# The seam between two layers of an attention and convolution kernel: the last head kept by quarters of partitions, one root table, a program order on three engines

## The chip, the cores and the metric

The kernel runs on one core of a Trainium2 chip, in float32. The metric is the device time of one execution in microseconds. A measurement is the median of several runs.

## The reference, cut to what matters

The input x has two images of 256 channels and 64 x 64 pixels. Two layers are applied, each to the group-normalised input (32 groups of 8 channels), and each is added to its input:

```python
x = x + layer0(_gn(x))
x = x + layer1(_gn(x))

def layer0(x):                      # attention over 4096 pixels, 8 heads of 32 channels
    q, k, v = qkv_w @ x + qkv_b
    return softmax(q.T @ k / sqrt(32)) @ v      # per head

def layer1(x):
    q, k, v = conv1 @ x + b1, conv2 @ x + b2, conv3 @ x + b3
    fq, fk = q / 8 + pos, k + pos
    # "lr": attention inside each of 64 blocks of 64 pixels taken 8 apart, then a 1x1 conv (lr_W), scale, shift, relu
    feats = relu(lr_W @ attention(blockify(fq), blockify(fk), blockify(v)) * scale + shift)
    # "sr": attention inside each 8x8 patch, behind two 1x1 convs with relu for q and k, sr_fv for v, sr_W after
    out_att = relu(sr_W @ attention(qx(feats), kx(feats), sr_fv @ feats) * scale + shift)
    # a 3x3 convolution of q, k and v, mixed by fc_w and dep_w
    out_conv = conv3x3(fc_w, dep_w, (q, k, v))
    return rate1 * out_att + rate2 * out_conv
```

The second group norm needs the mean and variance of the finished output of layer 0, all heads of a group of 8 channels and all pixels.

## The kernel before

The two images are worked one after the other (b = 0, 1). The 256 channels lie as two chunks (k = 0, 1) of 128 partitions, and the 4096 pixels as 8 tiles of 512; `xts[t]` holds tile t of x as 128 x 2 x 512.

*Attention of layer 0 (`attention0`).* A head and a half of the queries make a group g, 16 groups per image. Within a group a loop runs over 32 key blocks j, each with four units of 512 queries. For each unit PE computes scores (L438), ACT takes the exponential (L444), and PE multiplies by the values (L454). The four units of a group lie on four quarters of the partitions, 32 channels each. The sums of the exponentials over the keys are kept partly by adds on DVE (L491, tiles `e`), partly by adds in memory through DMAs that POOL issues (L501, `acc`). For the last group two more units (`SUMMED_LAST`) are left to PE, which adds up all of them over the partitions in the matmuls named `rows`. Earlier groups send their sums through DRAM (`dsum`, `dense`, `drec`) to be inverted and spread again, and send their result to `ctx0` in DRAM, from where `add_output` fetches it and adds it to x with the bias. PE, ACT and DVE run here in the order of the program (`tc.manual_schedule`). Elsewhere a scheduler orders engines by its own due times, apart from PE, whose order is by hand through the layer 1 code as well. `at_block(g, j, ...)` hangs a piece of work onto a block of this loop; `wanted` is a list of pieces that need a spare score bank in PSUM.

*The seam.* `finish_last` handles the last group without DRAM: reciprocal of `rows` (L557), then for each quarter a multiply (L563) and an add to x (L565) on 32 partitions. `Stats` makes the group norm: `bn_stats` by tile (L268), aggregation (L272), one matmul with a group matrix for the mean (`pm_l`, L273), four small DVE steps, one matmul for the variance (`pv_l`, L281), a square root on ACT (L282) and a reciprocal. For chunk 0 this happens at blocks 6 and 9 of the last group, for chunk 1 behind the last head. The square root and the exponential lie in different tables of ACT.

*The first part of layer 1 (`layer1_first`).* `to_groups` writes the normalised x in block order into `xg` (L980 on ACT, L295 on DVE). Chunk 0 is projected by PE first (L1011), then chunk 1, then position terms (L1015), for tile 0; then eight tiles of the block attention follow (scores `sp_lr` L910, values `pvs_lr` L893, `pc_lr` L948). For b = 0 `fold_products` multiplies two pairs of weight matrices first (transposes L208, copies L209, products L213, copies L216), and `conv_weights` prepares the weights of the convolution on DVE (L724 to L764, tile `prep`), stored by SP to `wf_kept` in DRAM (L766).

*The second part (`layer1_second`).* Tile by tile: the 8 x 8 attention (L1104, L1112, L948) and the convolution, whose weights are fetched from `wf_kept` (L781, `wf`) and for b = 0 turned by PE once (`pw`, L790). The convolution's matmuls are `mm` (L831).

*Buffers.* `w4` is a pool of 11 tiles of one size that all stages share. `es` (part of a ring of exponentials, and `acc[0]`), `xg` and `xp` share a single place, one after the other. `prep` and `wf` share another. [...]

Of the kernel before, what the change touches and what calls it, by code (L numbers as in the profile page):

```python
# [40 lines left out]
def direct_layers(ctx: ExitStack, tc: tile.TileContext, a: dict, out: bass.AP, bad: bass.AP):  # L41
# [17 lines left out]
    def w4(shape, name, dtype=F32):  # L59
        return work.tile(shape, dtype, tag="w4", name=name)  # L60
# [56 lines left out]
    nc.gpsimd.dma_start(out=bv0, in_=a["bv0"].rearrange("(k p) -> p k", p=P))  # L117

    wts = {}

# [56 lines left out]
    def stack_positions(t):  # L177
# [14 lines left out]
        return halves_of  # L192

    def fold_products():


        outer = {}
        wts["fv"] = w4([P, KC, C], "wt_fv")
        nc.gpsimd.dma_start(out=wts["fv"], in_=a["fv"].rearrange("(k p) m -> p k m", p=P))
        for name in ("lr", "srw"):  # L200
            outer[name] = w4([P, KC, C], "wt_" + name)
            nc.gpsimd.dma_start(out=outer[name], in_=a[name].rearrange("(k p) m -> p k m", p=P))
        for name, behind in (("w3", "lr"), ("fv", "srw")):
            turned = w4([P, KC, C], "turned_" + name)
            for j in range(KC):
                pt = bank([P, C], f"pt_{name}_{j}")
                for k in range(KC):
                    nc.tensor.transpose(pt[:, k * P : (k + 1) * P], wts[name][:, k, j * P : (j + 1) * P], ident)  # L208
                nc.vector.tensor_copy(turned[:, j, :], pt)  # L209
            for k in range(KC):  # L210
                pt = bank([P, C], f"pm_{name}_{k}")
                for j in range(KC):
                    nc.tensor.matmul(  # L213
                        pt, turned[:, j, k * P : (k + 1) * P], outer[behind][:, j, :], start=j == 0, stop=j == KC - 1
                    )
                nc.scalar.copy(wts[name][:, k, :], pt)  # L216
            nc.sync.dma_start(out=kept_w[name], in_=wts[name])
        pt = bank([P, KC], "pb_lr")
        for m in range(KC):
            for j in range(KC):  # L220
                nc.tensor.matmul(
                    pt[:, m : m + 1], outer["lr"][:, j, m * P : (m + 1) * P], wts["b3"][:, j : j + 1],
                    start=j == 0, stop=j == KC - 1,
                )
        moved = small.tile([P, KC], F32, tag="gn_d", name="moved")
        nc.vector.tensor_mul(moved, pt, vecs[:, V_LR : V_LR + 2])
        nc.vector.tensor_add(vecs[:, V_LR + 2 : V_LR + 4], vecs[:, V_LR + 2 : V_LR + 4], moved)


# [24 lines left out]
    class Stats:  # L254
# [11 lines left out]

        def tile(self, k, t):
            nc.vector.bn_stats(self.stats[:, k, t, :], self.xts[t][:, k, :])  # L268

        def means(self, ks, pm):  # L270
            for k in range(ks.start, ks.stop):
                nc.vector.bn_aggr(self.mv[:, k, :], self.stats[:, k].rearrange("p t s -> p (t s)"))  # L272
            nc.tensor.matmul(pm, group8, self.mv[:, ks, 0], start=True, stop=True)  # L273
            d = self.d[:, ks]
            nc.vector.tensor_copy(self.mean[:, ks], pm)
            nc.vector.tensor_sub(d, self.mv[:, ks, 0], self.mean[:, ks])
            nc.vector.tensor_mul(d, d, d)
            nc.vector.tensor_add(d, d, self.mv[:, ks, 1])

        def deviations(self, ks, pv):  # L280
            nc.tensor.matmul(pv, group8, self.d[:, ks], start=True, stop=True)  # L281
            nc.scalar.activation(self.rstd[:, ks], pv, AF.Sqrt, bias=eps)  # L282
            nc.vector.reciprocal(self.rstd[:, ks], self.rstd[:, ks])

    def group_stats(xts, tagn):
        st = Stats(xts, tagn)
        for t in range(NT):
            for k in range(KC):
                st.tile(k, t)
        st.means(slice(0, KC), bank([P, KC], f"pm_{tagn}"))  # L290
        st.deviations(slice(0, KC), bank([P, KC], f"pv_{tagn}"))
        return st.mean, st.rstd

    def normalise(dst, src, k, mean, rstd):
        nc.vector.tensor_scalar(dst, src, mean[:, k : k + 1], rstd[:, k : k + 1], ALU.subtract, ALU.mult)  # L295

# [97 lines left out]

    SUMMED_LAST = (NJ - 2, NJ - 1)

    def attention0(b, xts, held):
# [116 lines left out]
        def sum_rows(g, rows):  # L514
            if g == last:
                quarters(rows, ones, lambda u: acc[u], True, False)
                for j in SUMMED_LAST:
                    quarters(rows, ones, lambda u: unit(g, j, u), False, False)
            quarters(rows, ones, lambda u: added[g][u // 2][:, u % 2, :], g < last, True)
# [30 lines left out]
        def finish_last(g):  # L550

            h, p = divmod(g, 2)
            rows = psum["sc"].tile([P, 3, T], F32, tag="sa", name=f"rows_{b}")[:, 0, :]
            sum_rows(g, rows)
            avs = copied[g]
            kept = w4([P, T], f"kept_{b}")
            nc.vector.reciprocal(avs[:, 1, :], rows)  # L557
            nc.scalar.copy(kept, rows)
            row, c = slice(HD0 * (h % 4), HD0 * (h % 4) + HD0), h // 4
            o = [w4([P, 2, T], f"o_{b}_{g}_{w}") for w in range(2)]  # L560
            for u in range(4):
                q = slice(HD0 * u, HD0 * u + HD0)
                nc.vector.tensor_mul(o[u // 2][row, u % 2, :], avs[q, 0, :], avs[q, 1, :])  # L563
                xs = xts[4 * p + u][row, c, :]
                nc.vector.scalar_tensor_tensor(xs, o[u // 2][row, u % 2, :], bv0[row, c : c + 1], xs, ALU.add, ALU.add)  # L565

# [4 lines left out]

            return check

# [17 lines left out]
        def at_block(g, j, what):  # L591
            also.setdefault((g, j), []).append(what)
# [16 lines left out]
        wanted = []  # L609
        at_block(last, 6, lambda: wanted.append(lambda bank: st.means(first_chunk, bank[:, 0:1])))  # L610
        at_block(last, 9, lambda: wanted.append(lambda bank: st.deviations(first_chunk, bank[:, 0:1])))
        rests = {}
# [42 lines left out]
        with tc.manual_schedule(engines={E.PE, E.Activation, E.DVE}):  # L655
# [33 lines left out]
            assert next(work, None) is None  # L689
            return finish_last(last), st  # L690

# [271 lines left out]

    def layer1_first(b, xts, check, st):


        mean, rstd = st.mean, st.rstd

        xg = apool.tile([P, KC, 64, 8, 8], F32, tag="A", name=f"xg_{b}")
        shift = small.tile([P, KC], F32, tag="gn_shift", name=f"shift_{b}")  # L970

        def to_groups(k):
            nc.vector.scalar_tensor_tensor(
                shift[:, k : k + 1], mean[:, k : k + 1], -1.0, rstd[:, k : k + 1], ALU.mult, ALU.mult
            )
            for t in range(NT):
                dst = xg[:, k, :, t, :].rearrange("p (d e) o -> p d e o", d=8)
                src = xts[t][:, k, :].rearrange("p (d o e) -> p d e o", d=8, o=8)
                if k == 0 or t % 2:
                    nc.scalar.activation(  # L980
                        dst, src, AF.Identity, bias=shift[:, k : k + 1], scale=rstd[:, k : k + 1]
                    )
                else:
                    normalise(dst, src, k, mean, rstd)

# [36 lines left out]

        to_groups(0)
        if b == 0:
            fold_products()
        with tc.manual_schedule(engines={mybir.EngineType.PE}):
            open_tile(0)
            for m in range(KC):
                project(0, m, slice(0, 1))
            for t in range(NT):  # L1030
                st.tile(1, t)
            st.means(slice(1, KC), bank([P, 1], f"pm_l1_{b}"))
            st.deviations(slice(1, KC), bank([P, 1], f"pv_l1_{b}"))
            to_groups(1)
            check()
            for m in range(KC):
                project(0, m, slice(1, KC))
            for t in range(NT):
                def to_feats(m, pc, t=t):
# [17 lines left out]
        load_set(b, ("fq1", "fk1", "fv"))  # L1057
        if b == B - 1:
            report()
        if b == 0:  # L1060
            kept["bias"] = conv_weights()
        return feats, mean, rstd, shift

    def layer1_second(b, xts, feats, mean, rstd, shift, pacc):
# [28 lines left out]
        for t in range(NT):  # L1093
# [25 lines left out]
            with tc.manual_schedule(engines={mybir.EngineType.PE}):  # L1119
# [26 lines left out]
                if t < 2:  # L1146
                    conv()
            conv_edges(xts, t)
            results[t] = res
            for n in sorted(n for n in results if done >= 4 * (n // 2 + 1)):  # L1150
# [10 lines left out]
    for b in range(B):  # L1161
# [13 lines left out]
        with tc.tile_pool(name=f"sc_{b}", bufs=1, space=PSUM) as psum["sc"]:  # L1175
            check, st = attention0(b, xts, held)
        with tc.tile_pool(name=f"ps1_{b}", bufs=8, space=PSUM) as psum["ps"]:
            between = layer1_first(b, xts, check, st)
        with (
# [562 lines left out]
```

## Time and profile before

| | |
|---|---|
| time, median of 3 runs | 3227.35 us (3225.48 to 3230.16) |
| profiled execution, its own time | 3228.88 us |
| profiled execution, span of the instructions | 3227.1 us |
| granted clock of PE, mean | 0.984 |
| busy: PE, DVE, ACT, POOL | 3106.4, 2484.7, 2323.5, 822.5 us |

The profile gives busy time by engine, then the span in 40 slices of about 81 us each, then the groups of instructions by line. The timeline lists single instructions, with the idle time of the engine just before one in brackets and what ended it. The windows give busy time of all engines, granted clock, and DMA for a stretch.

### The profile page before, as it was taken

Reading aid. Unit: us, or ns where it says so; the run is one execution under the profiler, and the core shown is the slowest. Engines: PE = TensorE matmul, PEld = TensorE weight load, DVE = VectorE, ACT = ScalarE, POOL = GpSimd, SP = SyncE. Lnnn points to the kernel's source line nnn. Section 1 sums busy time; section 2 is a strip of 40 time slices with the busy share of each in tenths; the row PEclk is TensorE's granted clock in tenths of the full one; section 3 lists DMA queues with packets and bytes.
Section 4 is the critical chain, followed back from the end, with each engine's and each line's share of the span. In section 5 each row is a group of like instructions: output and inputs, shape, how many; then the busy total and the mean of one; then the engine's idle time right before and its main releaser. Section 6 shows DMA issues by size and latency. Waiting matters only on the chain. (4 is left out here: it accounts for less than half of the span.)

```text
span 3227.1 us, 62236 instructions
## 1 busy us (share of the span) xinstructions
PE 3106.4 (96%) x24873; PEld 1843.5 (57%) x24873; DVE 2484.7 (77%) x3230; ACT 2323.5 (72%) x2368; POOL 822.5 (25%) x913
## 2 busy tenths in 40 slices
PE   7999999999999969999998999999999999799998
PEld 4455555555555535667654555555555555356765
DVE  4699998999999888564436998989989998624543
ACT  2699999999999953522326999999999999524222
POOL 2122222222222210344201222222222222004430
PEclk9999999999999979999999999999999999799999
DMA  7968879689786641300159678796897866400000
GB/s 255 259 127 172 160 157 184 140 160 179 153 179 129 134 97 50 138 27 27 53 190 256 126 168 162 154 184 139 165 178 150 177 130 134 110 3 10 20 14 21
DMA packets 241868, 425.21 MB, mean 132 GB/s; under 512 B 98752, under 2 KB 109336, under 8 KB 239136
## 3 DMA queue, kind: packets, MB, share of 16 engines
q0 software_dynamic: 96288, 241.20, 38.7%
q1 hardware_dynamic: 145280, 179.93, 20.7%
q8 instruction: 197, 3.23, 0.4%
q14 instruction: 103, 0.84, 0.1%
HBM read 118.26 MB, written 67.86 MB: 58 GB/s over the span
## 5 line engine op out<-in xcount | busy, mean ns | idle before, releaser
L491 DVE TENSOR_TENSOR e<-e,es 128x1024 f32<-128x1024 f32 (+1 forms) x956 | 1040.6, 1146 | 92.6 <-ACT es L444 91.3
L454 PE MATMUL av<-es,v 128*32 128x256 f32 (+1 forms) x9644 | 747.4, 391 | 0.0
L491 DVE TENSOR_TENSOR e<-e,v 128x1024 f32<-128x1024 f32 (+1 forms) x640 | 676.5, 1111 | 53.2 <-ACT v L444 52.0
L444 ACT ACTIVATE es<-sa 128x1536 f32<-128x1536 f32 (+1 forms) x444 | 635.6, 1432 | 94.6 <-PE sa L438 52.2
L438 PE MATMUL sa<-q,k 128*128 128x512 f32 x1736 | 561.9, 431 | 16.2 <-ACT es L444 5.5
L454 PE MATMUL av<-v 128*32 128x256 f32 (+1 forms) x6228 | 507.0, 389 | 0.0
L454 PEld LDWEIGHTS av<-es,v 128*32 128x32 f32 x9644 | 316.9, 109 | 300.4 <-issue 162.0
L438 PEld LDWEIGHTS sa<-q,k 128*128 128x128 f32 x1736 | 280.5, 188 | 299.6 <-issue 142.4
L438 PE MATMUL sc<-q,k 128*128 128x512 f32 x1180 | 373.0, 397 | 9.6 <-ACT es L444 8.3
L438 PE MATMUL sb<-q,k 128*128 128x512 f32 x1180 | 371.5, 396 | 1.7 <-ACT es L444 1.5
L454 PEld LDWEIGHTS av<-v 128*32 128x32 f32 x6228 | 216.4, 109 | 178.6 <-issue 81.6
L444 ACT ACTIVATE es<-sc 128x1024 f32<-128x1024 f32 x296 | 306.9, 1037 | 7.1 <-DMA v<-es 7.1
L444 ACT ACTIVATE es<-sb 128x1024 f32<-128x1024 f32 x296 | 302.1, 1020 | 5.0 <-DMA acc<-es 5.0
L444 ACT ACTIVATE v<-sc 128x1024 f32<-128x1024 f32 x294 | 304.9, 1037 | 0.2 <-DMA acc<-v 0.2
L444 ACT ACTIVATE v<-sb 128x1024 f32<-128x1024 f32 x294 | 300.0, 1020 | 0.4 <-DMA acc<-v 0.4
L438 PEld LDWEIGHTS sc<-q,k 128*128 128x128 f32 x1180 | 211.1, 188 | 81.6 <-ACT es L444 19.7
L438 PEld LDWEIGHTS sb<-q,k 128*128 128x128 f32 x1180 | 221.1, 188 | 57.4 <-ACT es L444 5.0
L444 ACT ACTIVATE v<-sa 128x1536 f32<-128x1536 f32 (+1 forms) x146 | 209.2, 1433 | 33.4 <-PE sa L438 13.7
L831 PE MATMUL mm<-v,wf 128*128 128x256 f32 x1024 | 229.4, 383 | 2.5 <-DVE z L840 2.5
L501 POOL DMA_DIRECT2D es<-es x118 | 101.2, 857 | 484.4 <-ACT es L444 439.8
L821 POOL TENSOR_TENSOR v<-col 128x512 f32<-128x512 f32 x128 | 162.4, 1300 | 212.0 <-PE sp_sr L910 81.7
L831 PEld LDWEIGHTS mm<-v,wf 128*128 128x128 f32 x1024 | 194.7, 191 | 36.9 <-issue 7.7
(238 smaller groups left out, 3256.6 us busy)
## 6 DMA issues: line engine op xcount, KB each, us to landing
acc<-es POOLq DMA_DIRECT2D x130, 512.0 KB, 6.4
acc<-v POOLq DMA_DIRECT2D x84, 512.0 KB, 6.3
es<-es POOLq DMA_DIRECT2D x138, 256.0 KB, 4.3
v<-es POOLq DMA_DIRECT2D x134, 256.0 KB, 5.0
k<-wk_halves SPq DMA_DIRECT2D x64, 512.0 KB
q<-wq_halves SPq DMA_DIRECT2D x256, 128.0 KB
v<-v POOLq DMA_DIRECT2D x90, 256.0 KB, 4.9
es<-v POOLq DMA_DIRECT2D x86, 256.0 KB, 4.0
```

The costliest lines, as they stand in the source:

```text
L438: nc.tensor.matmul(sc[:, i, :], held["k", g // 2][:, j * P : (j + 1) * P], held["q", g, u // 2][:, u % 2, :], start=True, stop=True,)
L444: nc.scalar.activation(dst, sc[:, i : i + m, :], AF.Exp, scale=SC0)
L454: nc.tensor.matmul(dst[HD0 * u : HD0 * u + HD0, n], lhs, rhs(u)[:, n], start=start, stop=stop)
L491: nc.vector.tensor_add(dst[:, s, :], dst[:, s, :], src)
L501: nc.gpsimd.dma_start(out=dst, in_=src, accum_op=ALU.add)
L821: (nc.gpsimd.tensor_add if plus else nc.gpsimd.tensor_sub)(dst, rows(one), rows(two))
L831: nc.tensor.matmul(mm[:, m, r, :], wf[:, k, 4 * r + q, m * P : (m + 1) * P], v[r // 2][:, r % 2, k, :], start=k == 0, stop=k == KC - 1,)
```

## The change

The last group's output stays on the four quarters of the partitions: one multiply, one add and one `bn_stats` on 128 partitions take the place of four each. For this, the x and the bias of that head are fetched once more in that arrangement (`x_last`, `bv_last`); four small copies put the statistics into place, and four copies put the sum back into x, two on POOL and two on ACT. The other tiles of chunk 1 get their `bn_stats` inside the last group. The square root of chunk 0 moves from block 9 to behind the loop. Three units, not two, are left to PE's `rows`, and their order changes. PE, ACT and DVE are ordered by hand up to the projection of tile 0. For b = 0 the weights to be multiplied are fetched by SP at block 12 of the last group, and the copies of the turned ones go from DVE to ACT. The instructions of `conv_weights` on DVE are put behind the last normalisation. `report` moves to a later stage. The diff, cut:

```diff
+    bv_last = const.tile([P, 1], F32, name="bv_last")
+    for u in range(4):
+        nc.gpsimd.dma_start(
+            out=bv_last[HD0 * u : HD0 * u + HD0, :], in_=a["bv0"][C - HD0 : C].rearrange("(p o) -> p o", o=1)
+        )
...
-    def fold_products():
+    def fetch_to_fold():
         wts["fv"] = w4([P, KC, C], "wt_fv")
-        nc.gpsimd.dma_start(out=wts["fv"], in_=a["fv"].rearrange("(k p) m -> p k m", p=P))
+        nc.sync.dma_start(out=wts["fv"], in_=a["fv"].rearrange("(k p) m -> p k m", p=P))
         for name in ("lr", "srw"):
             outer[name] = w4([P, KC, C], "wt_" + name)
-            nc.gpsimd.dma_start(out=outer[name], in_=a[name].rearrange("(k p) m -> p k m", p=P))
+            nc.sync.dma_start(out=outer[name], in_=a[name].rearrange("(k p) m -> p k m", p=P))
+
+    def fold_products():
...
-                nc.vector.tensor_copy(turned[:, j, :], pt)
+                nc.scalar.copy(turned[:, j, :], pt)
+            yield
...
-    SUMMED_LAST = (NJ - 2, NJ - 1)
+    SUMMED_LAST = (NJ - 3, NJ - 2, NJ - 1)
...
             if g == last:
-                quarters(rows, ones, lambda u: acc[u], True, False)
                 for j in SUMMED_LAST:
-                    quarters(rows, ones, lambda u: unit(g, j, u), False, False)
+                    quarters(rows, ones, lambda u: unit(g, j, u), j == SUMMED_LAST[0], False)
+                quarters(rows, ones, lambda u: acc[u], False, False)
...
         def finish_last(g):
+            nc.scalar.activation(st.rstd[:, first_chunk], st.d[:, first_chunk], AF.Sqrt, bias=eps)
...
-            for u in range(4):
-                q = slice(HD0 * u, HD0 * u + HD0)
-                nc.vector.tensor_mul(o[u // 2][row, u % 2, :], avs[q, 0, :], avs[q, 1, :])
-                xs = xts[4 * p + u][row, c, :]
-                nc.vector.scalar_tensor_tensor(xs, o[u // 2][row, u % 2, :], bv0[row, c : c + 1], xs, ALU.add, ALU.add)
+            y = avs[:, 0, :]
+            nc.vector.tensor_mul(y, y, avs[:, 1, :])
+            nc.vector.scalar_tensor_tensor(y, y, bv_last, held["x_last"], ALU.add, ALU.add)
+            some = small.tile([P, 6], F32, tag="gn_some", name=f"some_{b}")
+            nc.vector.bn_stats(some, y)
+            for u in range(4):
+                nc.vector.tensor_copy(
+                    st.stats[P - HD0 : P, 1, 4 * p + u, :], some[HD0 * u : HD0 * u + HD0, :]
+                )
+
+            def put(copy, us):
+                for u in us:
+                    copy(xts[4 * p + u][P - HD0 : P, 1, :], y[HD0 * u : HD0 * u + HD0, :])
...
-        at_block(last, 6, lambda: wanted.append(lambda bank: st.means(first_chunk, bank[:, 0:1])))
-        at_block(last, 9, lambda: wanted.append(lambda bank: st.deviations(first_chunk, bank[:, 0:1])))
+        def variance_of_first(bank):
+            st.variances(first_chunk, bank[:, 0:1])
+            nc.scalar.copy(st.d[:, first_chunk], bank[:, 0:1])
+
+        at_block(last, 5, lambda: st.aggregate(first_chunk))
+        at_block(last, 6, lambda: wanted.append(lambda bank: st.means(first_chunk, bank[:, 0:1], nc.scalar.copy)))
+        at_block(last, 11, lambda: st.spread(first_chunk))
+        at_block(last, 12, lambda: wanted.append(variance_of_first))
+
+        for t in range(NT):
+            if t < NT // 2:
+                at_block(last, 27 + t, lambda t=t: st.tile(1, t))
+            else:
+                at_block(last, 16 + t, lambda t=t: st.tile(1, t, P - HD0))
+        if b == 0:
+            at_block(last, 12, fetch_to_fold)
...
+        at_block(last, 21, fetch_x_last)
...
-        to_groups(0)
-        if b == 0:
-            fold_products()
-        with tc.manual_schedule(engines={mybir.EngineType.PE}):
+        with tc.manual_schedule(engines={E.PE, E.Activation, E.DVE}):
+            st.aggregate(second)
+            fold = fold_products() if b == 0 else iter(())
+            put(nc.gpsimd.tensor_copy, (0, 1))
+            ahead = (1, 1, 1, 1, 0) if b == 0 else (0,) * 7
+            for t, n in enumerate(ahead):
+                to_groups(0, t, True)
+                for _ in range(n):
+                    next(fold)
+                if t == (3 if b == 0 else 4):
+                    put(nc.scalar.copy, (2, 3))
+            pm, pv = bank([P, 1], f"pm_l1_{b}"), bank([P, 1], f"pv_l1_{b}")
+            st.means(second, pm, nc.vector.tensor_copy)
+            st.spread(second)
+            st.variances(second, pv)
+            st.deviations(second, pv)
+            shift_of(st, 1)
+            for t in range(len(ahead), NT):
+                to_groups(0, t, True)
+            n_act = 1 if b == 0 else 2
+            for t in range(NT):
+                done = to_groups(1, t, t < n_act)
+            for _ in fold:
+                pass
+            check()
             open_tile(0)
             for m in range(KC):
                 project(0, m, slice(0, 1))
-            for t in range(NT):
-                st.tile(1, t)
-            st.means(slice(1, KC), bank([P, 1], f"pm_l1_{b}"))
-            st.deviations(slice(1, KC), bank([P, 1], f"pv_l1_{b}"))
-            to_groups(1)
-            check()
             for m in range(KC):
                 project(0, m, slice(1, KC))
+        with tc.manual_schedule(engines={E.PE}):
...
         if b == 0:
-            kept["bias"] = conv_weights()
+            with tc.issue_after(done.ins):
+                kept["bias"] = conv_weights()
```

## The prediction

> **What bounds the kernel now.** I read the busy table first, then the slices, then the chain of waits, then the timeline of the stretches where the chain leaves PE.
>
> ```profile
> PE 3106.4 (96%) x24873; PEld 1843.5 (57%) x24873; DVE 2484.7 (77%) x3230; ACT 2323.5 (72%) x2368; POOL 822.5 (25%) x913
> PE   7999999999999969999998999999999999799998
> PEclk9999999999999979999999999999999999799999
> ```
>
> PE is the bound nearly everywhere, so only three kinds of time are for sale: PE's idle, PE running at half clock, and work put on PE. Both rows dip in slices 15 and 35, the two seams. At batch 1's seam the chain has the whole story; the timeline of the same stretch gives the lengths:
>
> ```profile
> 2771.86 9.70 ACT L980 ACTIVATE xg<-x,shift,rstd_l 128x512 f32<-128x512 f32 x8 [1.18 <-PE rows L454]
> 2773.52 3.36 DVE L557 RECIPROCAL avs<-rows 128x512 f32<-128x512 f32 x1 [1.23 <-PE rows L454]
> 2782.07 2.08 PE L1011 MATMUL pq_lr<-xg,wt_w 128*128 128x512 f32 x2 [8.62 <-ACT kept L558]
> 2784.27 0.69 DVE L268 BATCH_NORM_STATS2 stats_l<-x 128x6 f32<-128x512 f32 x1
> 2791.90 0.59 PE L273 MATMUL pm_l<-mv_l,group 128*128 128x1 f32 x2 [3.24 <-DVE mv_l L272]
> 2793.99 1.28 ACT L282 ACT_TABLE_LOAD   x1 [11.97 <-PE pv_l L281]
> 2800.91 2.08 PE L1011 MATMUL pq_lr<-xg,wt_w 128*128 128x512 f32 x2 [7.01 <-ACT xg L980]
> 2811.82 0.48 PE L910 MATMUL sp_lr<-k_lr,q_lr 128*64 128x64 f32 x4
> ```
>
> PE waits 8.62 us for eight ACT xg and kept, runs the first chunk, waits 3.24 us for the slow statistics of the last head (per quarter 0.68 + 0.75 + 0.69, one behind another), then 7.01 us for table load, sqrt and the second chunk's xg. What PE does run there is cold:
>
> ```profile
> 2784.60:2787.90 3.30, 3.30 (x5) 1.35 (x4) 3.17 (x6) 0.00 (x0) 0.00 (x0) 0.50 0.03 11
> 2801.00:2811.80 10.80, 10.80 (x12) 3.05 (x12) 0.69 (x1) 2.48 (x3) 0.00 (x0) 0.50 0.00 0
> 1344.15:1347.57 3.42, 2.93 (x27) 2.69 (x26) 2.17 (x4) 2.88 (x6) 3.34 (x4) 1.00 0.02 5
> ```
>
> The third column from the end is the granted clock. A 128x512 pass costs 0.86 us at 0.50, 0.43 at 1.00. Stepping windows, the clock drops at 2777.7, rises at 2787.9 after a 3.4 us window wholly full of projections, drops at 2791.3, and rises only at 2818.6. Batch 0 has the same shape (1163.2 down, 1180.2 up, 1190.5 down, 1214.4 up), with the weight products in between. So a seam costs its gaps twice: once as idle, once as half speed of what follows.
>
> **The change part by part** (times of the profiled execution; span 3227.1, its own time 3228.88; the median of the runs is 1.5 below that, and I subtract gains from the median).
>
> *1. Root tables.* In the last group now:
>
> ```profile
> 2730.22 1.28 ACT L282 ACT_TABLE_LOAD   x1
> 2731.82 0.96 PE L438 MATMUL sa<-q,k 128*128 128x512 f32 x3 [1.28 <-ACT rstd_l L282]
> 2735.66 0.96 PE L438 MATMUL sa<-q,k 128*128 128x512 f32 x3 [0.52 <-ACT es L444]
> ```
>
> Add a third gap of 0.18 at 2737.49: PE loses 1.98 us per batch to the pair of loads. [...] What replaces it is two tiny copies on ACT from a spare bank; the next scores wait for each, some 0.3 us (the 0.26 of the sqrt row plus a hand-over): -1.98 + 0.6 = **-1.4 us per batch**. Bounds: 0 to -2.
>
> *2. Statistics in the last group.* Eight bn_stats of 0.69 = 5.5 us more on DVE, two adds of 1.15 less, against a DVE that idled 5.15 + 1.15 us at these same matmuls. The x and fold fetches pass SP, idle between 1121 and 1131, ahead of the results of group 14. Cost 0; without that cover, the difference of 3 us.
>
> *3. Rows.* One more unit is summed by PE: 5 groups of 0.86 us, not 4: +0.86. The acc slot, which the first xg waits for, is now read in the fourth of five groups instead of the first: xg may start at 2773.6, 1.7 later than 2771.9. This speaks against the change; it is in the sum below.
>
> *4. Batch 1's seam.* DVE after rows at 2774.4: reciprocal 3.4, mul 0.7, add 0.75, bn_stats 0.7, four small copies 0.7, aggregate 0.4: 2780.8 (now 2791.8). pm, four small DVE steps, pv, as now 1.9: variance at 2782.6. ACT: one root table at 2770.7, under the rows; from 2773.6 seven xg of 1.21, kept 0.6, two copies back 1.2 (the other two on POOL; nearest row, kept's 0.56, and up to 1.3 on POOL, waited for only by the last xg), sqrt 0.3, eighth xg: first projections at about **2785.0**, 2.9 later than 2782.07. Then the gain: the second chunk's xg (six on DVE at 0.67, two on ACT) end near 2788, while PE is still in the first chunk; the waits of 3.24 and 7.01 and the 1.28 table load go. PE runs two chunks without a pause: 8 cold passes of 0.86 are 6.9; the clock should rise after the first full window (3.4 to 6.8 us from the start), and the second chunk with its position passes takes 5 to 6 us warm. sp_lr at 2795.6 to 2797.3, against 2811.82: -14.5 to -16.2. From there to the next tile is now 8.24 us, of which about 2.5 is the cold clock (sp and pvs_lr take 5.7 in a warm tile). **-17.5 us.**
>
> [...] 6.9 us hold one full window of a 3.4 us grid, barely: I take the rise, at 0.75. Without it the gain is 2.5 + 5 + 1 less: about -9.
>
> *5. Batch 0's seam and what eats it.* The weight products are woven into the same order, turned copies on ACT (0.37 each), weights fetched at block 12 and not after the rows. The first projections come at 1176 to 1180 (now 1184.5), the second chunk follows at once (now 1197.4), sp_lr at 1188 to 1193 against 1208.3. So tile 1 starts 17 to 22 us earlier. But the conv weights are made on DVE beside this stage, and the change lets them begin only after the last normalise:
>
> ```profile
> 1164.59 0.63 DVE L724 TENSOR_TENSOR prep<-prep 128x108 f32<-128x108 f32 x3 [0.61 <-DMA prep<-in_bx_dram]
> 1216.07:1324.50 108.43, 108.43 (x585) 63.44 (x585) 95.39 (x249) 41.88 (x61) 2.28 (x3) 1.00 0.18 49
> 1330.13 0.35 SPq L781 DMA_DIRECT2D wf<-wf_kept  x1
> 1342.58 2.40 PE L790 MATMUL pw<-ident,wf 128*128 128x128 f32 x20 [0.82 <-DMA wf<-wf_kept]
> ```
>
> DVE is busy 95.4 us from 1216.1 to 1324.5; softmax and bd rows are 16.9 of it, so conv weights 78.5, a rate of 0.72. Before 1216 their rows add to 28.2; they overlap (14 of 478 ns within 5.62), so 23.7. Total 102 us of DVE. After: start 1179, alone till sp at 1188 (9 us), then at 0.72 until the stage's end at 1188 + 121 = 1309 (87 us), the last 6 alone: done at 1315, now 1324.4. With sp at 1193 it is 1319. From there stores, fetch and pw take 18.2 us as now: pw at 1333 to 1337 instead of 1342.6: 5.5 to 9.5 gained of some 20. PE ends prq near 1319 to 1324 and waits 13 us for wf. In that gap it goes cold, and pw's 64 transposes (7.3 us busy, 0.11 each) run at half speed. [...] By the trace they lift it: 1.7 to 3.4 us lost. [...] I take -7.5 + 2.5: **-5 us**, ends -9 and +3. Nothing else waits: POOL's loads for prep are issued as before, the loc_lr loads stand behind the stores as now.
>
> *6. Check and report moved.* Small DVE steps (0.7, 0.2) off the path: 0; bounds 0 and 1.
>
> Sum: -1.4 x 2 - 17.5 - 5 = **-25.3**; 3227.35 - 25.3 = **3202**.
>
> **The rivals.**
> A (0.62): as above, batch 1's seam gains in full, batch 0's is mostly handed to the wait for wf: 3195 to 3209.
> B (0.20): the clock does not rise in batch 1's first chunk, or the woven products run cold and late (ACT now does turned copies, xg and pm copies in order): -2.8 - 9 - 1 = -13: about 3214. For it: the long cold stretches above. Against: two full windows in each seam did lift it.
> C (0.10): conv weights are no bound, since DVE, no longer stalled in the seam, is faster than 0.72: both seams pay, -2.8 - 17.5 - 18: about 3189. For it: DVE idles 11 us before nm, den and bd rows in that window.
> D (0.05), slower: the fold fetches. They stand in SP's queue ahead of group 14's denominators, waiting for slots that PE frees. DVE's order is fixed: if dense comes late, the reciprocals and x adds at block 26 stall the row sums behind them, and the score ring fills. Slots freed at the rows of group 14 cost nothing. Scores of seven units come every 3.5 to 3.7 us and a block has four, so a block is 2.1 us, and that is the price of each block of lateness. It decides from 12 blocks (25 us) on: held from block 12 to the group's end, 20 blocks, it costs 42, net +17: 3244. Against: SP's queue shows no wait of that kind and PE frees slots every group.
> E (0.03): the seam does not move, since xg starts later by the shared slot (part 3) and the hand order leaves ACT waiting for quarters; only part 1 stays, some -3 + 2: 3226.
>
> **How the numbers follow.** Predicted time 3202. Leaving out C's lower half, D and E and the tail of B gives 3190 to 3215. Within 0.2% is 6.5 us, about what a measurement here can tell from no change. Faster A + B + C = 0.92, same E 0.03, slower D 0.05.
>
> **What would show it.** Right: no table load around 2730 and PE's gaps there down to 0.3; bn_stats of the last head once, not four times; sp_lr of batch 1 within 27 us of the rows' end (now 38.4); no PE gap between the two chunks; the granted clock at 1.00 from before sp_lr on; in batch 0 a PE gap of 10 to 15 us ahead of pw, ended by the DMA of wf. Wrong: a gap before pm_l or before the second chunk; clock 0.50 up to pvs_lr (B); no gap ahead of pw (C); waits in group 15 (D).

## The result, and the profile after

The changed kernel takes 3211.94 us (median of 4, 3209.81 to 3213.45) against 3228.76 before in the same runs: ratio 0.9949, 95% interval 0.9931 to 0.9966, so 16.8 us faster. 3202 was forecast, with 3190 to 3215 as the range. The profiled execution has a span of 3211.4 us and a granted clock of 0.989.

The page of the changed kernel, busy table and slices:

```profile
PE 3093.3 (96%) x24889; PEld 1838.3 (57%) x24889; DVE 2487.2 (77%) x3223; ACT 2316.5 (72%) x2371; POOL 826.7 (26%) x918
PE   7899999999999989699998999999999999899998
PEclk9999999999999999899999999999999999999999
```

The dip of image 1's seam (35th slice) is an 8 instead of a 7, that of image 0's (15th) an 8 instead of a 6, and the clock's dips there are gone (9 in both slices). But the 17th slice, a 9 before, is now a 6, and the clock dips in it: an idle time has moved there. The timeline of image 1's seam, first two lines of before, then the same stretch after:

```profile
2769.84 0.59 PE L454 MATMUL rows<-es,ones 128*32 128x512 f32 x1
2820.06 1.88 PE L1011 MATMUL pq_lr<-xg,wt_w 128*128 128x512 f32 x4
...
2772.56 1.90 PE L482 MATMUL rows<-es,ones 128*32 128x512 f32 x16
2773.40 1.28 ACT L584 ACT_TABLE_LOAD   x1
2776.24 6.13 ACT L1042 ACTIVATE xg<-x,shift,rstd_l 128x512 f32<-128x512 f32 x5 [1.25 <-PE rows L482]
2782.01 0.69 DVE L599 BATCH_NORM_STATS2 some<-avs 128x6 f32<-128x512 f32 x1
2784.43 0.56 PE L288 MATMUL pm_l<-mv_l,group 128*128 128x1 f32 x2 [7.39 <-DVE mv_l L285]
2786.54 0.24 ACT L301 ACTIVATE rstd_l<-pv_l,eps 128x1 f32<-128x1 f32 x1
2788.02 2.08 PE L1072 MATMUL pq_lr<-xg,wt_w 128*128 128x512 f32 x2 [1.61 <-ACT xg L1042]
2791.50 1.02 PE L1072 MATMUL pq_lr<-xg,wt_w 128*128 128x512 f32 x2
2799.02 0.34 PE L977 MATMUL sp_lr<-k_lr,q_lr 128*64 128x64 f32 x4
2804.49 1.88 PE L1072 MATMUL pq_lr<-xg,wt_w 128*128 128x512 f32 x4
```

One load of the root table, one bn_stats of the last head, and from 2788.02 on PE does not stop before the scores: the second chunk follows the first, and a pair of passes falls from 2.08 to 1.02 us after 3.5 us. From the first rows matmul (2772.56) to the first projection of tile 1 (2804.49) is 31.9 us; before it was 2820.06 - 2769.84 = 50.2. So this seam gives 18.3 us.

Image 0's seam gives as much: rows at 1155.87, tile 1 at 1196.50, 40.6 us against 59.2 (1156.91 to 1216.07). But here is what follows it, PE's timeline from the second branch on:

```profile
1318.51 3.70 PE L1194 MATMUL prq_sr<-hq_sr,wt_fq 128*128 128x512 f32 x8 [0.37 <-ACT hq_sr L1026]
1346.00 9.61 PE L857 MATMUL pw<-ident,wf 128*128 128x128 f32 x64 [23.79 <-DMA wf<-wf_kept]
1355.44 1.89 PE L898 MATMUL mm<-v,wf 128*128 128x256 f32 x8
```

PE is done with prq 19.6 us earlier than before (1322.2, not 1341.8), waits 23.8 us for the convolution's weights, and starts pw 3.4 us later than before (1342.58). What happened to the weights is on DVE, with POOL beside it. First the end of the weights and the start of POOL's transforms before, then the same stretch after:

```profile
1323.30 1.10 DVE L764 TENSOR_TENSOR prep<-prep 128x256 f32<-128x256 f32 x3
1335.37 2.13 POOL L817 TENSOR_TENSOR col<-xp 128x1152 f32<-128x1152 f32 x1 [6.04 <-ACT xp L1074]
...
1315.16 0.42 DVE L829 TENSOR_TENSOR prep<-prep 128x256 f32<-128x256 f32 x1
1316.36 2.36 DVE L830 TENSOR_TENSOR prep<-prep 128x256 f32<-128x256 f32 x1
1318.65 2.03 DVE L826 TENSOR_TENSOR prep<-prep 128x768 f32<-128x768 f32 x1
1320.60 2.89 DVE L829 TENSOR_TENSOR prep<-prep 128x256 f32<-128x256 f32 x2
1323.41 3.77 DVE L830 TENSOR_TENSOR prep<-prep 128x256 f32<-128x256 f32 x2
1327.10 4.26 DVE L831 TENSOR_TENSOR prep<-prep 128x256 f32<-128x256 f32 x3
...
1315.82 2.62 POOL L884 TENSOR_TENSOR col<-xp 128x1152 f32<-128x1152 f32 x1 [6.03 <-ACT xp L1156]
1318.52 6.09 POOL L888 TENSOR_TENSOR v<-col 128x512 f32<-128x512 f32 x4
1324.69 2.20 POOL L884 TENSOR_TENSOR col<-xp 128x1152 f32<-128x1152 f32 x1
```

The same 128x256 add takes 0.42 us at 1315.16 and 1.4 to 2.4 from the moment POOL begins the transforms of the convolution's image. Before, POOL began these at 1335.37, when the last weight (1324.40) had long been made. The ordering puts the weights later, the gain of the seam puts POOL's work earlier, and the two now lie on top of each other: the last weight is made at 1331.4. The next section tests this.

### The profile page after: what moved, and what is told of

It is laid out like the page before. It is cut to its first block, busy times and chain, and to the rows that moved or that the text cites. A ratio compares the mean times of both kernels' runs of the same rounds, so it can differ in the third digit from the quotient of the medians.

```text
span 3211.4 us, 62287 instructions
## 1 busy us (share of the span) xinstructions
PE 3093.3 (96%) x24889; PEld 1838.3 (57%) x24889; DVE 2487.2 (77%) x3223; ACT 2316.5 (72%) x2371; POOL 826.7 (26%) x918
## 5 line engine op out<-in xcount | busy, mean ns | idle before, releaser
L472 ACT ACTIVATE v<-sa 128x1536 f32<-128x1536 f32 (+1 forms) x146 | 209.2, 1433 | 35.0 <-PE sa L466 14.9
```

The source lines that it names most:

```text
L472: nc.scalar.activation(dst, sc[:, i : i + m, :], AF.Exp, scale=SC0)
```

## The experiments

Each was timed in rounds with the kernel before on the same chip; the ratios are to it, with their 95% intervals. Differences between two variants that are smaller than these intervals are read from the traces. A time "from the rows" is counted from the first rows matmul of that image.

**POOL held back.** One DVE copy of one element per partition makes POOL's first transform wait for the last weight.

```diff
+        kept["last"] = new_cols[:, 3, 0, 0:1]
...
         one, two, plus = terms[q]
+        if (b, s, q) == (0, 0, 0):
+            nc.vector.tensor_copy(col[:, 0, 0, 0:1], kept["last"])
```

> The changed kernel, with one tiny DVE copy added that makes the first transform of the convolution's image on POOL wait until the last conv weight is made on DVE. Theory (POOL's transforms, which now start at 1315.8, block the last adds of two SBUF operands on DVE): the last rows of prep fall back from 1.4 to 2.4 us each to 0.34 to 0.9, prep ends near 1320 and not at 1331.4, the wait of PE ahead of pw shrinks from 23.8 to about 12.5, and the time falls by about 11, to 3201. Rival (DVE is late by its amount of work alone, or by the DMA stores beside it): those rows stay as long, pw stays at 1346, and the time is 3212 or, with POOL later, up to 3215.

Measured: 3203.46 us, ratio 0.9929 (0.9911 to 0.9947). The DVE timeline shows the adds at their old length, and PE's the shorter wait:

```profile
1317.85 0.95 DVE L826 TENSOR_TENSOR prep<-prep 128x768 f32<-128x768 f32 x1
1318.72 0.76 DVE L829 TENSOR_TENSOR prep<-prep 128x256 f32<-128x256 f32 x2
1319.39 0.76 DVE L830 TENSOR_TENSOR prep<-prep 128x256 f32<-128x256 f32 x2
1320.06 1.09 DVE L831 TENSOR_TENSOR prep<-prep 128x256 f32<-128x256 f32 x3
...
1324.60 5.48 PE L1197 MATMUL prq_sr<-hq_sr,wt_fq 128*128 128x512 f32 x8 [5.30 <-ACT hq_sr L1029]
1338.51 8.82 PE L858 MATMUL pw<-ident,wf 128*128 128x128 f32 x64 [8.43 <-DMA wf<-wf_kept]
```

The weights are done at 1321.2; counted from the rows, which come 1.2 later in this execution, that is 11.4 us earlier than in the changed kernel. pw starts 8.7 earlier in the same count: the stores and the fetch behind the weights took 17.4 us here, 14.6 in the changed kernel. By time, 8.5 us between the medians where 11 was expected, the two kernels are not told apart, since the intervals overlap. The timelines decide, and they are as the theory has it: with POOL's start moved, the adds are back at 0.42 us each, though the DMA stores of the weights still run beside them (SP issues twelve from 1310.70 on). So neither the amount of DVE's work nor the stores made them long. ACT's order changed too (twelve xp rows ahead of hq_sr), which gives the new wait of 5.3 ahead of prq. It costs nothing here, since PE waits for wf behind it anyway.

**Weights without their ordering.**

```diff
-            with tc.issue_after(done.ins):
-                kept["bias"] = conv_weights()
+            kept["bias"] = conv_weights()
```

> The changed kernel without the ordering that puts the conv weights on DVE behind the last normalisation: the scheduler weaves them into the seam, from about 1164. Theory: some 9 us of their work are done in DVE's gaps before 1181, so prep ends near 1311, ahead of POOL's transforms at 1315.8; pw near 1328 and not 1346; the seam itself is 0.5 to 1 us later; time 3212 - 17 = 3195. Rival (the ordering protects the seam, whose small DVE steps get stuck behind prep): sp_lr of batch 0 is 5 us later or more, and the time falls by less than 10.

Measured: 3195.54 us, ratio 0.9902 (0.9886 to 0.9918). sp_lr of image 0 comes 36.6 us after the rows (35.4 with the ordering), so the ordering protects 1.3 us of the seam. The weights are done at 1316.3, not the 1311 expected, but ahead of POOL's first transform at 1318.96; pw starts at 1332.8. Counted from the rows, mm of image 0 starts 14.5 us earlier than in the changed kernel, though the seam is 1.3 longer:

```profile
1315.86 0.43 DVE L831 TENSOR_TENSOR prep<-prep 128x256 f32<-128x256 f32 x1
1318.96 2.14 POOL L884 TENSOR_TENSOR col<-xp 128x1152 f32<-128x1152 f32 x1 [6.63 <-ACT xp L1155]
1332.82 9.57 PE L857 MATMUL pw<-ident,wf 128*128 128x128 f32 x64 [7.41 <-DMA wf<-wf_kept]
```

So the ordering, one part of the change, saves 1.3 us at the seam and costs 15.8 behind it; the two ratios to before differ by 0.0047, 15 us.

**Half of the sums left out**, as a ceiling: `range(12)` becomes `range(6)` in the loop over summands of a tap. The sums are then not those of the reference. In fact 108 instructions and 45 us of DVE go, not the 99 and 39 of the expectation.

> The changed kernel with half of the twelve summands of each convolution tap left out, 99 instructions of 0.4 us on DVE in batch 0: 39 us less work, so that the conv weights are in time. It gives the ceiling of the seam. Theory: no wait ahead of pw, PE warm there, time 3212 - 23.4 - 1.7 = 3187. Rival (another wait stands right behind, such as POOL's transforms ahead of the first mm, or the fetch itself): 3195 or more, with a PE gap ahead of mm.

Measured: 3185.06 us, ratio 0.9874 (0.9858 to 0.9890). PE goes into pw without a gap, and the 64 rows of pw take 7.47 us (9.61 in the changed kernel); the granted clock of the whole execution is 0.993:

```profile
1316.52 3.70 PE L1194 MATMUL prq_sr<-hq_sr,wt_fq 128*128 128x512 f32 x8 [1.07 <-ACT hq_sr L1026]
1320.05 7.47 PE L857 MATMUL pw<-ident,wf 128*128 128x128 f32 x64
```

The wait for wf is gone, and no other stands between prq and mm.

**The root tables alone**, on the kernel before: the square root of chunk 0 behind the loop, ACT's two copies, and nothing else of the change.

```diff
+            nc.scalar.activation(st.rstd[:, first_chunk], st.d[:, first_chunk], AF.Sqrt, bias=eps)
             rows = psum["sc"].tile([P, 3, T], F32, tag="sa", name=f"rows_{b}")[:, 0, :]
...
-        at_block(last, 9, lambda: wanted.append(lambda bank: st.deviations(first_chunk, bank[:, 0:1])))
+        at_block(last, 11, lambda: st.spread(first_chunk))
+        at_block(last, 12, lambda: wanted.append(variance_of_first))
```

> The kernel before with one part of the change alone: the square root of chunk 0 moves behind the last head, mean and variance are copied by ACT. Theory: the PE gaps of 1.98 us per image around the two table loads shrink to about 0.5, 1.4 gained per image; but the table load now stands ahead of the first xg, 0.7 us later than now, and moves the seam by that: net -0.7 per image, 3227 - 1.4 = 3225.5. Rival (the gain inside the last group is larger, since also the score ring had run empty): 3 us per image.

Measured: 3219.32 us, ratio 0.9979 (0.9971 to 0.9987), 7.0 us and not 1.4. The rival's 3 per image is near in size, but not for its reason: from the row sums of group 14 to the first rows matmul the last group of image 1 takes 56.6 us and not 58.8, 2.2 less (image 0 the same), where 3 was claimed. The rest is at the seam, which I had expected to lose 0.7. ACT's timeline of image 1 shows why it wins there:

```profile
2763.11 1.28 ACT L570 ACT_TABLE_LOAD   x1
2764.41 0.30 ACT L570 ACTIVATE rstd_l<-d_l,eps 128x1 f32<-128x1 f32 x1
2785.77 0.26 ACT L299 ACTIVATE rstd_l<-pv_l,eps 128x1 f32<-128x1 f32 x1 [10.38 <-PE pv_l L298]
```

The first load lies under the rows, and the second square root, which is on the path, finds its table loaded; before, a load of 1.28 us stood ahead of it. From rows to tile 1 the seam is 2.5 us shorter in image 0 and 3.3 in image 1. In image 0 the reason is another: there the load lay in an idle time of ACT already before, six us ahead of the root at 1190.42. But on DVE the reciprocal that follows the root had five of the weights' adds just ahead of it and now has two, and the second chunk's first xg waits 0.68 and not 1.74 us. That is the scheduler's order, not the table. Two lines of before, then one of this run:

```profile
1184.25 1.28 ACT L282 ACT_TABLE_LOAD   x1
1192.42 4.92 ACT L980 ACTIVATE xg<-x,shift,rstd_l 128x512 f32<-128x512 f32 x4 [1.74 <-DVE shift L973]
...
1189.30 4.92 ACT L1006 ACTIVATE xg<-x,shift,rstd_l 128x512 f32<-128x512 f32 x4 [0.68 <-DVE shift L999]
```

These four stretches give 10.2 us, and the two profiled executions differ by 10.7. The medians differ by 7.0 (4.2 to 9.4 by the interval of the ratio), so some of it is scatter between executions. Alone, this small part brings about 7 us, where the whole change brings 16.8.

**The quarters undone** in the changed kernel: four multiplies and adds on 32 partitions, and four bn_stats of whole tiles. The fetch of `x_last`, the copies back and the four bn_stats of the other 96 partitions inside the last group fall away with it. Cut:

```diff
-            nc.vector.tensor_mul(y, y, avs[:, 1, :])
-            nc.vector.scalar_tensor_tensor(y, y, bv_last, held["x_last"], ALU.add, ALU.add)
...
-            nc.vector.bn_stats(some, y)
...
+            for u in range(4):
+                q = slice(HD0 * u, HD0 * u + HD0)
+                nc.vector.tensor_mul(o[u // 2][row, u % 2, :], avs[q, 0, :], avs[q, 1, :])
+                xs = xts[4 * p + u][row, c, :]
+                nc.vector.scalar_tensor_tensor(xs, o[u // 2][row, u % 2, :], bv0[row, c : c + 1], xs, ALU.add, ALU.add)
+                st.tile(1, 4 * p + u)
```

> The changed kernel with one part undone: the last head's output goes into x by four multiplies and four adds on 32 partitions and four bn_stats of whole tiles, as before; the hand order stays. Theory: three times 2.1 us more on DVE less the four small copies, so pm of image 1 comes 5 later; the hand order holds the last xg of chunk 0 behind the square root, so the first projections move with it, less 1.2 us of copies on ACT: sp_lr of image 1 4 to 5 us later. In image 0 pm waits for the weight products anyway (DVE idle 5.97 before it), nothing moves. Time 3212 + 4.5 = 3216.5. Rival (the bn_stats inside the last group were what cost; or the quarters were what freed the whole seam): 3212 or less, or 3222 and more.

Measured: 3222.69 us, ratio 0.9982 (0.9973 to 0.9990), 10.8 slower than the change, where 4.5 was expected. In image 1 sp_lr comes 32.8 us after the rows, not 26.5: 6.3, of which 5.5 is the later start of the projections (20.9 us after the rows, not 15.5) and the rest lies between them and sp_lr. The rest arises in image 0, where I expected nothing: mm starts 7.5 us later from the rows. (Of this, 2.9 is made up at a later mm, where PE waits 2.46 and not 3.67 us; in the changed kernel the 32 mm behind this wait take 8.83 us, with the clock at 0.50 for part of them, and 32 mm right behind pw take 7.07 here. The run with two units below gains the same 2.9 without such a shift, so it may be scatter.) There the seam itself is indeed unchanged (sp_lr 35.2 after the rows, 35.4 with the quarters), but the weights' adds came out later and all twelve lie beside POOL:

```profile
1318.67 1.92 DVE L822 TENSOR_TENSOR prep<-prep 128x768 f32<-128x768 f32 x1
1333.71 5.11 DVE L829 TENSOR_TENSOR prep<-prep 128x256 f32<-128x256 f32 x3
...
1353.55 9.94 PE L855 MATMUL pw<-ident,wf 128*128 128x128 f32 x64 [30.02 <-DMA wf<-wf_kept]
```

The twelve take 20 us here, 17 in the changed kernel, 5.7 with POOL held back. They begin 4.4 us later than in the changed kernel, and PE waits 6.2 us longer for wf.

**Two units and acc first**, as before, in the changed kernel: `SUMMED_LAST` with two blocks, `acc` ahead of the units.

> The changed kernel with two units left to the rows and acc summed first, as before. Theory: xg starts 1.7 us earlier, PE has 0.86 less, but ACT's order then waits for the variance: the first projections of image 1 come 0.5 to 0.9 earlier, image 0 is bound by wf: 3211. Rival (DVE's two more adds end behind the units, and the last rows wait for them): rows end 1 us later or more, 3213.

Measured: 3207.83 us, ratio 0.9938 (0.9922 to 0.9955). Its interval overlaps that of the change, so by time this part is not told apart, though the medians differ by 4.1 us in its favour. In the trace of image 1, rows end 0.85 us earlier and the first projections come 14.9 us after the rows' start, not 15.5, as expected; sp_lr is then no earlier (26.6 and 26.5), for a third pair of passes took 1.67 us, and 1.02 in the changed kernel. The first xg starts only 0.6 us earlier, not 1.7. The reordering of the rows is worth nothing that these runs show.

**pw behind the k branch**, with POOL held back, and with the weights without their ordering. In image 0's first tile, pw and the first conv step go behind the k branch and the scores.

```diff
-                if t == 0:
+                late = b == 0 and t == 0
+                if t == 0 and not late:
                     wf = fetch_conv_weights(b)
-                if t + 1 < NT:
+                if t + 1 < NT and not late:
                     conv()
...
                 next(parts)
+                if late:
+                    wf = fetch_conv_weights(b)
                 if t + 1 < NT:
                     conv()
...
-                if t < 2:
+                if t < 2 or (b == 0 and t == 2):
                     conv()
```

> The kernel in which POOL waits for the last conv weight, with the same later place for pw. Theory: the 8.4 us gap ahead of pw is filled, and pw runs warm (8.8 to 7.4 us): 3203.5 - 9.5 = 3194. Rival: POOL, which starts its transforms at 1321, sets the pace then, and the gain is under 5.

> The changed kernel without the ordering of the conv weights behind the last normalisation, and with pw and the first conv step of image 0 put behind the k branch and the scores of its first tile; the conv step left out there is made up two tiles later. It may beat both kernels. Theory: PE has 7.2 us of k branch and about 5 of scores and values to do while wf is on its way, so the gap of 7.4 us ahead of pw and the 1.8 us of cold transposes go: 3195.5 - 9.2 = 3186, close to the 3185 of the half-sum kernel. Rival (the conv steps crowd later, where mm waits for its single accumulator or for POOL): 3191 or more.

Measured: 3195.85 us (ratio 0.9898, 0.9881 to 0.9914) with POOL held back, and 3187.95 us (ratio 0.9875, 0.9858 to 0.9891) without the ordering. The second is the fastest complete kernel here, 24 us under the change and 40.8 under before:

```profile
1317.96 3.60 PE L1193 MATMUL prq_sr<-hq_sr,wt_fq 128*128 128x512 f32 x8
1321.40 3.60 PE L1185 MATMUL phk_sr<-feats,wt_fk 128*128 128x512 f32 x8
1330.09 1.15 PE L977 MATMUL sp_sr<-rk_sr,rq_sr 128*64 128x64 f32 x32
1331.17 4.75 PE L857 MATMUL pw<-ident,wf 128*128 128x128 f32 x40
```

PE has work until wf is there, and the 64 rows of pw take 7.6 us (4.75 and 2.84) and not 9.61; the granted clock of the whole execution is 0.991. By the ratios (0.9875, and 0.9874 with half of the sums left out) nothing that can be measured is left to the ceiling. Both kernels are within 2 us of what was expected. With POOL held back the wait of 5.3 us ahead of prq is still there, and no longer hidden behind another.

## Why the prediction was right or wrong

The direction and the range were right; the size was 25.3 forecast, 16.8 measured. That the time fell into the range is in part luck: 3212 lies outside the 3195 to 3209 of the favoured case A and next to the 3214 of B, and B's mechanism, a clock that does not rise, did not come. Step by step, in the prediction's numbering:

1. *Root tables*, -1.4 per image forecast. The gaps were sized right: they went from 1.98 to 0.49 in image 1 (0.30 and 0.19) and 0.37 in image 0. The last group became 2.1 shorter in either image, though; the further 0.6 was not traced to a row. On its own this part is worth about 7 us: in image 1 the seam's own table load belongs to it, which the forecast had under step 4, and in image 0 the order on DVE changed with it.
2. *Statistics in the last group*, 0: right, no other gap appeared there.
3. *Rows*, later start of xg: right as a mechanism (xg waits 1.25 us for the rows now too), but mis-sized: undone, it gives back 0.6 us at the first xg and not 1.7.
4. *Image 1's seam*, -17.5: 18.3 from rows to tile 1. The first projections came 15.5 us after the rows' start, where the sum had 15.2 (its own terms, added again, give 15.5). The clock rose after 3.4 us of the first chunk:

```profile
2788.00:2791.20 3.20, 3.18 (x4) 1.51 (x5) 3.20 (x6) 2.40 (x2) 0.00 (x0) 0.50 0.07 13
2791.30:2794.70 3.40, 3.40 (x9) 1.25 (x8) 1.66 (x6) 0.01 (x1) 0.00 (x0) 0.99 0.00 0
```

   The third column from the end is the granted clock. The grid of 3.4 us fits the changes of the clock in the traces: those before that the prediction lists lie 10.2, 3.4 and 27.3 us apart in image 1 (3, 1 and 8 times 3.4), and in the changed kernel the clock fell at 1176.9 and 2781.1 and rose 6.8 and 10.2 us later, at 1183.7 and 2791.4. That a wholly busy window lifts it is shown by no run; before, the clock stayed at 0.50 from 2801.0 to 2811.8 with PE's row busy for all 10.8 us, and in the changed kernel it rose 3.6 and 3.4 us after the first projection, the early end of the 3.4 to 6.8 forecast. Rival B, a rise that fails, did not come, in either seam: in image 0 a pair of passes falls to 1.03 us at 1183.70, 3.6 us after the first. Of the 18.3, the quarters are 6.3 (undone) and the roots 3.3 (alone). The rest, some 8.7 if the parts add, was not taken apart: no run undoes the hand order on ACT and DVE alone.
5. *Image 0's seam*, -5: this step failed. Its first half was right: sp_lr at 1191.2 (1188 to 1193 forecast), the weights bind, PE waits (23.8 us, where 13 was forecast) and goes cold (the clock is at 0.50 from 1327.1 on), and rival C is out. The failing term is "done at 1315 ... With sp at 1193 it is 1319": they were done at 1331.4. The amount of DVE work was sized well, since with POOL held back they are done at 1321.2 (1320.0 by the rows of the changed kernel, against some 1318 for sp_lr at 1191). What the sum left out is POOL: it said "Nothing else waits" and looked only at POOL's loads, not at its transforms, which start when the stage ends and so moved 19.5 us forward, onto the last adds. That made the last weight 11.4 us later; with POOL held back, mm comes 3.3 us earlier than before from the rows, near to the 5 of the forecast. In the changed kernel, from the last weight to pw took 14.6 us and not 18.2. In all, mm starts 6.2 us later, counted from the rows, instead of 5 earlier: 11.2 us, more than the whole miss (8.5 by the medians, 9.0 by the sum of stretches below). Steps 1 and 4 made up 2.2 of it by giving more than their forecasts.

   The lengths of the rows show how far this goes: DVE's add on `prep` (128x256) goes from 0.42 to about 1.48 us (up to 2.36) beside POOL's transforms, near to the length of one POOL row there (v, 1.32 to 1.98), and back to 0.42 when POOL is held. Why they lengthen was not shown; the trace has only the lengths. Not every DVE row lengthens: `wf<-pw`, which reads PSUM, takes 0.69 us before, with POOL busy 8.21 of 8.40 us around it, and 0.69 in the changed kernel with POOL idle.

   The forecast for the transposes held. In the changed kernel pw starts at half clock, with nothing but transposes on PE:

```profile
1346.00:1349.30 3.30, 3.30 (x16) 3.30 (x17) 1.14 (x2) 0.60 (x1) 0.00 (x0) 0.50 0.00 0
1351.00:1351.50 0.50, 0.50 (x6) 0.50 (x5) 0.26 (x1) 0.23 (x1) 0.00 (x0) 1.00 0.00 0
1353.70:1355.40 1.70, 1.70 (x18) 1.70 (x17) 1.34 (x3) 1.19 (x2) 0.00 (x0) 1.00 0.00 0
```

   The clock is at 1.00 from 1351.0 on, after 5.0 us of transposes and before any mm has run: pw to mm takes 9.4 us and not 7.75, 1.7 lost, the lower end of the 1.7 to 3.4 in the forecast. The step's end of +3 is reached only if some 8.5 us are lost to a cold clock (-5.5 + 8.5); no run shows such a loss, and these 1.7 are what the changed kernel showed in its place.
6. *Check and report*: nothing seen of them.

Together, from the profiled executions: -2.1 twice, -18.3, +6.2 from rows to mm in image 0 are -16.3; the spans differ by 15.7. The remaining 0.6 is a balance of stretches that the change does not touch: image 0 behind mm is 1.3 longer, nearly all of it at one later mm (a wait of 3.67 us, 2.47 before), and the attention stages differ by up to 1.6 between the two executions.

## What to carry to other kernels

When a stage becomes shorter, list everything that its end releases, on every engine, and ask what that will now run beside; here DVE's 128x256 adds took 1.4 to 2.4 us beside POOL's transforms, and 0.42 alone. A reordering that protects one path (the ordering of the weights: 1.3 us) has to be priced by what it puts back (15.8 us). And where PE must wait for a transfer, look first for independent matmuls that the program order has placed behind the wait.

## What the runs showed of the hardware

Beside POOL's transforms DVE's 128x256 adds of the weights took 3.5 times as long (0.42 to about 1.48 us), and with POOL held back they took 0.42 again; the transforms themselves lengthened far less (four v rows 6.09 us beside the adds, 4.9 alone). And PE's clock rose from 0.50 to 1.00 in the changed kernel with transposes alone on PE: they start at 1346.0, and the granted clock is 1.00 from 1351.0 on.
